# A hybrid of selective scan, attention and experts on one core: the scan's input product moved next to its scan, and PSUM divided anew

## The chip, the cores and the metric

The kernel runs on one core of a Trainium2 chip. The metric is the device time of one execution in microseconds. TensorE is called PE, VectorE DVE, ScalarE ACT and GpSimd POOL in the profile; SP is the engine that issues most of the loads. PSUM, the memory into which PE writes, has eight banks here of 128 partitions x 512 float32.

## The reference

Four images of 384 channels and 32 x 32 points pass through two layers. The first is a group norm and a selective scan along four directions (rows, columns, and both reversed), followed by a layer norm over channels, a GELU and a residual. The second takes the 1024 points as tokens: causal attention with one head of 384, then four experts of which two are taken for each token, each behind a layer norm and with a residual. The change touches the scan alone:

```python
x_dbl = jnp.einsum('bkdl,kcd->bkcl', xs, x_proj_weight)
dts, Bs, Cs = (x_dbl[:, :, :R], x_dbl[:, :, R:R + N], x_dbl[:, :, R + N:])
dts = jnp.einsum('bkrl,kdr->bkdl', dts, dt_projs_weight)
dt = jax.nn.softplus(dts + dt_projs_bias[None, :, :, None])

def step(h, inp):
    dtt, ut, bt, ct = inp
    dA = jnp.exp(dtt[..., None] * A)
    h = h * dA + (dtt * ut)[..., None] * bt[:, :, None, :]
    y = jnp.einsum('bkdn,bkn->bkd', h, ct)
    return (h, y)
```

There are B = 4 images, K = 4 directions, D = 384 channels, N = 16 states and L = 1024 steps, all in float32.

## The kernel before

**Units.** A unit of the scan holds 32 channels x 4 states on the 128 partitions, and all 1024 steps along the free dimension. It is named by image b, direction k, block m of 128 channels, quarter q of the states and j, a block of 32 channels in m: 4 x 4 x 3 x 4 x 4 = 768 units. j runs innermost, so four units in a row have the same b, k, m and q; they share one tile bc, in which B and C of four states are spread over the partitions, and their results meet in one set of matmuls. Two directions (0 and 2, or 1 and 3) make a stage of 96 units; there are two for each image, eight in all.

**What a unit does.** `front` (line 263) has ScalarE compute da = exp(dt * A) (line 268) and VectorE the product v = (dt * u) * B (line 270), which goes into PSUM, two banks for each v. `middle` (line 279) is VectorE's scan, h = da * h + v along the steps (line 282); directions 2 and 3 run it backwards. `back` (line 288) has GpSimd multiply h by C in place (line 290). Behind the fourth unit of a group it issues eight short matmuls, four for each half of the steps (the profile shows two instructions for each), that add the states up into y (line 299), in PSUM, two banks. When a block m of a stage is complete, `evict` has VectorE add y to the image's tile yb (lines 366 and 372).

**The order.** `push` (line 312) writes the order out by hand. Called with unit t it runs `front` of t, then `back` of t-2, then `middle` of t-1:

```python
flow.append(t)
done = front(t) if t is not None else None
if len(flow) > 2 and flow[-3] is not None:
    back(flow[-3], done)
if len(flow) > 1 and flow[-2] is not None:
    middle(flow[-2], done)
```

`done` is VectorE's product of unit t. `order` puts two edges: GpSimd's product of t-2 waits for it by a semaphore ("beside a scan"), and the scan of t-1 stands behind it in VectorE's queue without a semaphore ("the next unit's product first"). So VectorE runs v of t, scan of t-1, v of t+1, scan of t, and GpSimd's product of t-2 lies beside the scan of t-1. Two calls of `push(None)` empty the pipeline at the end.

The framework's scheduler turns this program into one queue for each engine. It follows these edges and the edges of data, places the rest by its own model, and puts in every semaphore; an operation that waits for several engines gets separate semaphore instructions of the engine's sequencer ahead of it.

**Preparation.** While a stage runs, the next one is prepared in small pieces: `todo` is a list of functions, and one is called after every eighth unit (line 393). `project_x` computes x_dbl for a direction (six matmuls, line 214, and copies by ScalarE, line 217); `project_dt` computes dt for a block m (two matmuls, line 229, two softplus on ScalarE, line 232, and dt * u on VectorE, line 233) and stores both to DRAM from ScalarE's queue (line 234). SP reads them back spread over four partitions each (dt4 and du4, line 246, six buffers each), and bc likewise (line 257, three buffers). `groupnorm` and `finish` (layer norm, GELU, residual) of an image are pieces too. All their PSUM tiles come from the pool `ps_m`, one bank each, by the tag "pm".

**Buffers.** da has three, h eight, bc three. PSUM's eight banks are divided among y (one tile of two banks), v (two tiles of two banks) and `ps_m` (two tiles of one bank).

Of the kernel before, what the change touches and what calls it, by code (L numbers as in the profile page):

```python
# [12 lines left out]
PSUM = bass.MemoryType.PSUM  # L13
# [27 lines left out]
def hybrid_kernel(  # L41
# [59 lines left out]
    with ExitStack() as ph:  # L101
# [6 lines left out]
        dap = ph.enter_context(tc.tile_pool(name="s_da", bufs=3))  # L108
        scr = ph.enter_context(tc.tile_pool(name="s_scr", bufs=4, space=DRAM))
        ps_y = ph.enter_context(tc.tile_pool(name="s_psy", bufs=1, space=PSUM))  # L110
        ps_b = ph.enter_context(tc.tile_pool(name="s_psb", bufs=2, space=PSUM))
        ps_m = ph.enter_context(tc.tile_pool(name="s_psm", bufs=2, space=PSUM))

        def load_x(b):
            xn = one.tile([P, M, L], F32, tag="xn", name=f"xn_{b}")
# [147 lines left out]
        def front(t):  # L263
            b, k, m, q, j = t["at"]
            g = m * NJ + j
            name = t["name"] = f"{b}_{k}_{g}_{q}"
            t["da"] = dap.tile([P, L], F32, tag="da", name=f"da_{name}")
            nc.scalar.activation(t["da"], t["dt4"], AF.Exp, scale=a4[:, k * NG + g, q : q + 1])  # L268
            t["v"] = ps_b.tile([P, L], F32, tag="v", name=f"v_{name}")
            return nc.vector.tensor_tensor(t["v"], t["du4"], t["bc"][:, 0, :], ALU.mult)  # L270

        def order(ins, after, how, reason):
            if after is not None:
                tc.add_manual_dep(
                    ins.ins, after.ins.name,
                    mybir.DependencyInfo(how, mybir.DependencyReason.DATA), reason=reason,
                )

        def middle(t, after):
            step = -1 if t["at"][1] >= 2 else 1  # L280
            t["h"] = hp.tile([P, L], F32, tag="h", name=f"h_{t['name']}")
            scan = nc.vector.tensor_tensor_scan(  # L282
                t["h"][:, ::step], t["da"][:, ::step], t["v"][:, ::step], 0.0,
                op0=ALU.mult, op1=ALU.add,
            )
            order(scan, after, mybir.DependencyClass.NoSync, "the next unit's product first")

        def back(t, after):
            h, j = t["h"], t["at"][4]
            product = nc.gpsimd.tensor_tensor(h, h, t["bc"][:, 1, :], ALU.mult)  # L290
            order(product, after, mybir.DependencyClass.Sync, "beside a scan")
            done_h.append(h)
            if j == NJ - 1:

                first = None
                for half in range(NH):
                    s = bass.ts(half, 512)
                    for jj in (NJ - 1, *range(NJ - 1)):
                        mm = nc.tensor.matmul(  # L299
                            t["y"][jj * DJ : (jj + 1) * DJ, s], sel, done_h[jj][:, s],  # L300
                            start=t["first"], stop=t["last"], tile_position=(0, jj * DJ),
                        )
                        order(mm, first, mybir.DependencyClass.NoSync, "one row of matmuls")
                        first = mm
                done_h.clear()
            if t["then"] is not None:
                t["then"]()

        flow = []
        done_h = []  # L310

        def push(t):

            flow.append(t)
            done = front(t) if t is not None else None
            if len(flow) > 2 and flow[-3] is not None:
                back(flow[-3], done)
            if len(flow) > 1 and flow[-2] is not None:
                middle(flow[-2], done)

        state = {}

# [36 lines left out]
        for si, (b, pair) in enumerate(stages):  # L359
# [18 lines left out]
            for m in range(M):  # L378
                y = ps_y.tile([P, L], F32, tag="y", name=f"y_{b}_{pair}_{m}")
                for k in PAIRS[pair]:  # L380
                    dt4 = [spread_dt(b, k, m * NJ + j) for j in range(NJ)]
                    for q in range(NQ):
                        bc = spread_bc(b, k, m, q)
                        for j in range(NJ):
                            last = k == PAIRS[pair][1] and q == NQ - 1
                            push(dict(
                                at=(b, k, m, q, j), dt4=dt4[j][0], du4=dt4[j][1], bc=bc, y=y,
                                first=k == PAIRS[pair][0] and q == 0, last=last,
                                then=(lambda m=m, y=y, f=evict: f(m=m, y=y))
                                if last and j == NJ - 1 else None,  # L390
                            ))
                            count += 1
                            if count % 8 == 4 and todo:
                                todo.pop(0)()
        push(None)
        push(None)
        for f in todo:
            f()
# [5 lines left out]
    with ExitStack() as ph:  # L404
# [4 lines left out]
        ps_m = ph.enter_context(tc.tile_pool(name="a_psm", bufs=2, space=PSUM))  # L409
# [104 lines left out]
    with ExitStack() as ph:  # L514
# [4 lines left out]
        ps_m = ph.enter_context(tc.tile_pool(name="f_psm", bufs=1, space=PSUM))  # L519
# [193 lines left out]
```

## Time and profile before

| | us |
|---|---|
| median of two runs | 5710.09 (5709.13 to 5711.04) |
| the profiled execution | 5708.17 |
| its span | 5706.4 |
| up to the first units of the scan | 62 |
| scan stage | 2926 |
| last image's finish | 64 |
| attention | 498 |
| experts | 2156 |

The five stretches are cut at 62, 2988, 3052 and 3550 us of the span, by eye from the timeline. Over the span PE is busy for 3614.5 us, VectorE for 3239.4, GpSimd for 1928.0 and ScalarE for 1656.5. In the scan stage VectorE is busy for 2883.53 of 2926 us, GpSimd for 1801.85, ScalarE for 1249.82 and PE for 987.46, at a granted PE clock of 0.58.

In the profile, a group of instructions is named by its line, engine and operation and by the tiles that it writes and reads; behind that stand the number of instructions, their busy time and the mean of one in ns, then the idle time of the engine just before them and what ended most of it. The timeline lists start and duration of single instructions in microseconds. An operation that is held up in the middle, by a port that another engine holds, counts as busy for all of that time. "DVEq" or "POOLq" is an engine's sequencer, which waits for semaphores and hands operations to the engine.

### The profile page before, as it was taken

The page shows a single profiled execution, that of the slowest core. Times are in us where ns is not written, and L with a number is a line of the kernel's source. Part 1 is how long each engine was busy: PE and PEld are TensorE (multiplying, and loading weights), DVE is VectorE, ACT ScalarE, POOL GpSimd, SP SyncE. Part 2 cuts the span into 40 slices and gives each one's busy share as a digit, 9 for nine tenths or more (in the row PEclk, how much of TensorE's full clock was granted, in tenths as well). Part 3 has the DMA queues.
Part 4 walks back from the last instruction along what each step waited for, and adds up shares of the span by engine and source line. Part 5 has one row for each costly group of instructions (what it writes and reads, how often), then busy time and mean ns, then how long its engine had stood idle before and what let it go on. Part 6 is the DMA issues. An engine that isn't in the chain of part 4 may idle for free.

```text
span 5706.4 us, 29398 instructions
## 1 busy us (share of the span) xinstructions
PE 3614.5 (63%) x10144; PEld 1443.3 (25%) x10144; DVE 3239.4 (57%) x2174; ACT 1656.5 (29%) x1709; POOL 1928.0 (34%) x872
## 2 busy tenths in 40 slices
PE   5324333243342432422227998799999999999999
PEld 1001000010000100100003444444444444444444
DVE  6999999999999999999993332300000000000000
ACT  4435435344353453543321211111111111111111
POOL 3665656656556566566660000000000000000000
PEclk7556565565565655655558999699999999999999
DMA  6444435345344444444321001000000000000000
GB/s 212 155 162 160 153 136 203 137 164 181 125 179 175 145 168 158 155 165 159 127 103 53 11 11 66 1 0 0 0 33 0 0 33 0 0 0 6 11 11 17
DMA packets 149695, 510.62 MB, mean 89 GB/s; under 512 B 21661, under 2 KB 29725, under 8 KB 148521
## 3 DMA queue, kind: packets, MB, share of 16 engines
q1 hardware_dynamic: 124544, 442.55, 22.1%
q10 hardware_dynamic: 25000, 66.19, 3.1%
q8 instruction: 79, 1.29, 0.1%
q14 instruction: 72, 0.58, 0.0%
HBM read 443.68 MB, written 65.01 MB: 89 GB/s over the span
## 4 chain that ended last, share of the span: by engine, by line
PE 46%; DVE 35%; issue 13%; DMA 3%; ACT 1%; POOL 1%; SPq 0%; DVEq 0%; ACTq 0%; POOLq 0%
DVE h L282 28%; PE ph L605 17%; PE fy L631 17%; DVE v L270 4%; PE pqk L447 2%; PE po L504 2%; PE ss L474 2%; DMA du<-dts 1%; PE pv L459 1%; POOL h L290 1%; DMA bc<-rows 1%; PE var_ff L90 1%; PE pg L553 1%; DMA dt<-dts 1%; DVE dt L233 1%
## 5 line engine op out<-in xcount | busy, mean ns | idle before, releaser
L290 POOL TENSOR_TENSOR h<-h,bc 128x1024 f32<-128x1024 f32 x768 | 1808.0, 2354 | 1184.8 <-DVE v L270 1147.0
L299 PE MATMUL y<-h,sel 128*32 128x512 f32 x3072 | 679.1, 1026 | 1704.0 <-POOL h L290 1703.8
L282 DVE TENSOR_TENSOR_SCAN h<-da,v 128x1024 f32<-128x1024 f32 x768 | 1746.1, 2274 | 1.2 <-ACT da L268 1.2
L268 ACT ACTIVATE da<-dt,a 128x1024 f32<-128x1024 f32 x768 | 881.2, 1148 | 1608.6 <-DVE h L282 1583.5
L638 DVE SCALAR_TENSOR_TENSOR fo<-fy,b2s,tw 128x512 f32<-128x512 f32 x96 | 72.1, 751 | 1837.6 <-PE fy L631 1817.8
L270 DVE TENSOR_TENSOR v<-du,bc 128x1024 f32<-128x1024 f32 x768 | 1045.5, 1361 | 32.0 <-DMA du<-dts 8.7
L605 PE MATMUL ph<-fxn,w1s 128*128 128x512 f32 x2304 | 1053.8, 594 | 0.0
L631 PE MATMUL fy<-ht,w2s 128*128 128x512 f32 x2304 | 1051.5, 593 | 0.0
L641 POOL TENSOR_TENSOR t<-t,fo 128x512 f32<-128x512 f32 x96 | 118.9, 1267 | 2539.2 <-DVE fo L638 2539.2
L610 ACT ACTIVATE ht<-ph,b1s 128x512 f32<-128x512 f32 x384 | 263.8, 687 | 1737.9 <-PE ph L605 1737.9
L299 PEld LDWEIGHTS y<-h,sel 128*32 128x32 f32 x3072 | 113.0, 156 | 2234.1 <-POOL h L290 1986.2
L605 PEld LDWEIGHTS ph<-fxn,w1s 128*128 128x128 f32 x2304 | 439.5, 191 | 551.1 <-issue 551.1
L631 PEld LDWEIGHTS fy<-ht,w2s 128*128 128x128 f32 x2304 | 436.3, 190 | 534.7 <-issue 534.7
L229 PE MATMUL pdt<-xd,wdt 12*128 12x512 f32 x192 | 163.5, 956 | 134.8 <-ACT dt L232 117.1
L447 PE MATMUL pqk<-axn,wqkv 128*128 128x512 f32 x288 | 132.9, 623 | 13.9 <-DVE axn L94 13.9
L268 ACT ACT_TABLE_LOAD x100 | 128.3, 1283 | 5.6 <-DVE yb L338 3.9
L232 ACT ACT_TABLE_LOAD x88 | 112.9, 1283 | 11.3 <-DVE dt L233 5.5
L229 PEld LDWEIGHTS pdt<-xd,wdt 12*128 12x128 f32 x192 | 42.5, 267 | 268.2 <-ACT dt L232 214.9
L504 PE MATMUL po<-pt,vt 128*128 128x512 f32 (+3 forms) x288 | 101.2, 502 | 1.6 <-DVE t L508 1.6
L474 PE MATMUL ss<-kt,qt 128*128 128x512 f32 (+3 forms) x288 | 100.7, 487 | 0.0
L447 PEld LDWEIGHTS pqk<-axn,wqkv 128*128 128x128 f32 x288 | 57.5, 201 | 89.3 <-issue 89.3
L454 DVE COPY kt<-pqk 128x512 f32<-128x512 f32 x24 | 16.6, 692 | 108.9 <-PE pqk L447 108.9
(117 smaller groups left out, 1575.2 us busy)
## 6 DMA issues: line engine op xcount, KB each, us to landing
bc<-rows SPq DMA_DIRECT2D x384, 512.0 KB, 4.5
dt<-dts SPq DMA_DIRECT2D x192, 512.0 KB, 5.9
du<-dts SPq DMA_DIRECT2D x192, 512.0 KB, 5.7
dts<-dt ACTq DMA_DIRECT2D x48, 1024.0 KB, 4.4
w1s<-in_w SPq DMA_DIRECT2D x4, 2304.0 KB, 9.0
w2s<-in_w SPq DMA_DIRECT2D x4, 2304.0 KB, 9.2
xn<-in_x SPq DMA_DIRECT2D x4, 1536.0 KB, 6.6
xr<-in_x ACTq DMA_DIRECT2D x12, 512.0 KB, 4.1
```

The lines of the kernel that those rows point to most:

```text
L229: nc.tensor.matmul(ps, wdt[:, k, m * P : (m + 1) * P], xd[:R, s], start=True, stop=True)
L268: nc.scalar.activation(t["da"], t["dt4"], AF.Exp, scale=a4[:, k * NG + g, q : q + 1])
L270: return nc.vector.tensor_tensor(t["v"], t["du4"], t["bc"][:, 0, :], ALU.mult)
L282: scan = nc.vector.tensor_tensor_scan(t["h"][:, ::step], t["da"][:, ::step], t["v"][:, ::step], 0.0, op0=ALU.mult, op1=ALU.add,)
L290: product = nc.gpsimd.tensor_tensor(h, h, t["bc"][:, 1, :], ALU.mult)
L299: mm = nc.tensor.matmul(t["y"][jj * DJ : (jj + 1) * DJ, s], sel, done_h[jj][:, s], start=t["first"], stop=t["last"], tile_position=(0, jj ...
L447: nc.tensor.matmul(ps, wqkv[:, j, c, m * P : (m + 1) * P], xn[:, c, s], start=(c == 0), stop=(c == M - 1),)
L474: nc.tensor.matmul(ss[:, o:e], qt[:, c, i * P : (i + 1) * P], kt[:, c, o:e], start=(c == 0), stop=(c == M - 1),)
L504: nc.tensor.matmul(po[:, o:], vt[:, j, m * P : (m + 1) * P], pt[:, j, o:], start=(j == 0), stop=(j == nj - 1),)
L605: nc.tensor.matmul(ph_, w1s[:, c, f * P : (f + 1) * P], xn[:, c, h * 512 : (h + 1) * 512], start=(c == 0), stop=(c == M - 1),)
L610: nc.scalar.activation(ht, ph_, AF.Gelu, bias=b1s[:, e, f : f + 1])
L631: nc.tensor.matmul(acc["y"][m], w2s[:, f, m * P : (m + 1) * P], ht, start=(f == 0), stop=(f == NF - 1),)
```

## The change

The pool of v gets one buffer in place of two, and the pool of the preparation gets the two banks: four in place of two. With one buffer the product of unit t+1 overwrites what the scan of unit t reads, so it can't be issued ahead of that scan, and `push` is rewritten: called with unit t it runs `front` of t, `back` of t-1 and `middle` of t itself, with no edge for the scan's place in the queue. GpSimd's product of t-1 still waits for VectorE's product of t. One call of `push(None)` at the end is enough.

VectorE's order becomes v of t, scan of t, v of t+1, scan of t+1; GpSimd's product of t-1 lies beside the scan of t. No operation is added or removed, and the sizes are the same.

```diff
-        ps_b = ph.enter_context(tc.tile_pool(name="s_psb", bufs=2, space=PSUM))
-        ps_m = ph.enter_context(tc.tile_pool(name="s_psm", bufs=2, space=PSUM))
+        ps_b = ph.enter_context(tc.tile_pool(name="s_psb", bufs=1, space=PSUM))
+        ps_m = ph.enter_context(tc.tile_pool(name="s_psm", bufs=4, space=PSUM))
...
             flow.append(t)
             done = front(t) if t is not None else None
-            if len(flow) > 2 and flow[-3] is not None:
-                back(flow[-3], done)
             if len(flow) > 1 and flow[-2] is not None:
-                middle(flow[-2], done)
+                back(flow[-2], done)
+            if t is not None:
+                middle(t, None)
...
         push(None)
-        push(None)
```

## The prediction

> **What bounds the kernel now.** I read the stretches first, then the groups of the scan stage, then its timeline unit by unit, and last the chain at its end. The table by stretch gives the scan stage 2926 of 5706 us, with VectorE busy for 2883.53 of them; attention and the experts behind it (498 and 2156 us, PE at 457 and 2113) hold nothing that the change edits.
>
> ```profile
> 62.00:2988.00 2926.00, 987.46 (x3584) 216.91 (x3584) 2883.53 (x1684) 1249.82 (x1116) 1801.85 (x766) 0.58 0.45 158
> ```
> ```profile
> L290 POOL TENSOR_TENSOR h<-h,bc 128x1024 f32<-128x1024 f32 x768 | 1808.0, 2354 | 1184.8 <-DVE v L270 1147.0
> L282 DVE TENSOR_TENSOR_SCAN h<-da,v 128x1024 f32<-128x1024 f32 x768 | 1746.1, 2274 | 1.2 <-ACT da L268 1.2
> L270 DVE TENSOR_TENSOR v<-du,bc 128x1024 f32<-128x1024 f32 x768 | 1045.5, 1361 | 32.0 <-DMA du<-dts 8.7
> ```
>
> The columns of the first row, from the table by stretch, are its bounds, length, busy time (and instructions) of PE, weight loads, VectorE, ScalarE, GpSimd, then clock and DMA; the others are groups of the page (busy, mean ns of one | idle before, releaser). VectorE looks like the bound: no wait to speak of stands before its product or its scan. The timeline of two units (start, duration; a release in brackets) says more.
>
> ```profile
> 1499.68 1.36 DVE L270 TENSOR_TENSOR v<-du,bc 128x1024 f32<-128x1024 f32 x1
> ...
> 1500.95 2.27 DVE L282 TENSOR_TENSOR_SCAN h<-da,v 128x1024 f32<-128x1024 f32 x1
> 1501.18 2.34 POOL L290 TENSOR_TENSOR h<-h,bc 128x1024 f32<-128x1024 f32 x1 [1.23 <-DVE v L270]
> 1503.26 1.35 DVE L270 TENSOR_TENSOR v<-du,bc 128x1024 f32<-128x1024 f32 x1
> ...
> 1506.84 1.35 DVE L270 TENSOR_TENSOR v<-du,bc 128x1024 f32<-128x1024 f32 x1
> ```
>
> Three things. (1) A unit takes 1503.26 - 1499.68 = 3.58 us. (2) The scan starts 0.09 us *before* the product ahead of it ends (1499.68 + 1.36 = 1501.04 against 1500.95): nothing ties the two, they belong to different units. The next product starts 0.04 us *after* the scan ends, since it overwrites what that scan read. So on VectorE a neighbour that must be waited for costs 0.12 us over one that need not. (3) GpSimd's product starts 0.14 us after v ends and outlasts the scan: at 1503.26 it has 0.26 us to go. Over all units v takes 1.22 us where GpSimd is done, 1.29 with 0.19 us of overlap, 1.35 with 0.26, 1.46 with 0.37, 1.65 with 0.56: v = 1.22 + (overlap - 0.12). VectorE stands still, though "busy", until GpSimd lets go. The real loop is therefore 2.34 (GpSimd) + 1.23 (its idle time, the part of v after it lets go and the 0.14) = 3.57; the scan lies beside it. Bare VectorE work is 1.22 - 0.09 + 2.27 + 0.04 = 3.44. Of four units one costs 3.685: the first with a new bc, before which GpSimd checks two more semaphores (idle time 1.32). A group of four is 3 x 3.577 + 3.685 = 14.42 us, 192 times.
>
> **The change, part by part.**
>
> *Scan t right behind its own product.* No operation is added; v of unit t moves behind scan t-1, and only the neighbours differ. Between v and scan there now is a dependence, so -0.09 becomes a gap s, and VectorE's loop is 1.22 + s + 2.27 + 0.04 = 3.53 + s. GpSimd's loop stays 3.57: the product of t-1 still waits for v of t and still lies beside a scan. The larger loop wins, so s is free up to 0.04 and costs in full above.
>
> How large is s? The trace's records of the semaphore instructions show that every scan already waits for a PE count (release of its h buffer) in a separate sequencer step, and for ScalarE's da on the instruction itself; one in four waits for GpSimd too. None waits for its own v: the next product's wait covered that. The last scan, behind which no product follows, does: its separate step holds VectorE's count and PE's together. So after the change the wait for v sits in the sequencer's step ahead of every scan, not on the instruction. Such steps are dear when nothing covers them:
>
> ```profile
> 68.70 0.02 DVEq L270
> 68.72 0.04 issue
> 68.76 0.06 DVE v L270
> ```
> ```profile
> 2985.60 1.47 DVE v L270
> 2987.07 0.02 issue
> 2987.09 0.02 POOLq L290
> 2987.11 0.09 issue
> 2987.20 6.96 POOL h L290 x3
> ```
>
> In the chain of waits, VectorE needs 0.04 from the end of its step to the start of the operation; v's count is seen 0.02 to 0.04 after v's end; a step with two semaphores takes 0.05 where the trace has one. So s = 0.03 + 0.05 + 0.04 = 0.12. A scan with a fourth wait has a second step, 0.06 to 0.07 more by GpSimd's rows (its two steps lie 0.06 apart). Bounds: at least 0.04, the plain wait between scan and v (below that the scan would read an unfinished product); at most 0.24, what GpSimd needs with three steps. I take 0.12, from VectorE's own rows.
>
> Queued behind the waiting scan on VectorE: the next product, and behind that GpSimd's product and ScalarE's da, all of which move with it.
>
> Sum for a group at s = 0.12: two units of 3.65 (+0.075 each), the one with the fourth wait 3.72 (+0.14), and the first with a new bc, where GpSimd still outlasts the scan: it ends 0.24 + 2.36 = 2.60 after v, the next v starts at 0.12 + 2.31 = 2.43, overlap 0.17, v 1.27, unit 3.70 (+0.015). Together +0.305, times 192 = **+59 us**.
>
> The Trainium skill speaks against this cost: "VectorE: DVE Perf Modes", section "The DRAIN you can't avoid", says that a semaphore between chained VectorE operations costs nothing extra. By that rule the scan would follow its product as closely as a stranger, GpSimd's loop would stay the bound, and the sum for the units would be 0. The trace's 0.04 against -0.09 speaks for the measurement.
>
> *One unit less in flight.* At the end three GpSimd products run after the last v (6.96 us); now it is two: -2.3 us. At the start the first scan (65.80) waits behind the second product, which waits for a DMA (64.66); it can now run at 62.5, and one product and scan leave the path: about -3.
>
> *Operations put between units* (42 products of dt, 24 additions of y): each lengthens GpSimd's idle time from 1.23 to about 2.37 (1.14), and in a loop bound by VectorE costs 1.26 - 0.07 - 0.08 - 0.04 = 1.07: -0.07 x 66 = -5 us. One that lands between v and its scan even hides s.
>
> *ScalarE's da* has three buffers before and after; da of t waits for scan t-3, and three products and two scans lie between the two either way, some 8.4 us. Its 1.15 us with a softplus and two table loads (1.28 + 0.69 + 1.28) fits: 0. If it did not, the row of VectorE waiting for da (1.2 us now) would show it.
>
> *The queues.* SP's bc loads follow GpSimd's fourth product of a group (1507.13 against its end at 1507.10); that stays, with one product less between v and release. The order of SP's issues, and ScalarE's store of dts, are as before; GpSimd issues no DMA. 0.
>
> *Four banks for the preparation.* PE waits 117 us for ScalarE before the dt matmuls. PE is busy for a third of this stage and nothing on VectorE waits for it there; at the start some 2 us may go (two copies of x_dbl wait 2.40 and 2.00 for PE). I count 0, bounds -5 and 0. Two softplus halves may then share their table loads; ScalarE has room, 0.
>
> Sum: +59 - 2 - 3 - 5 = +49. The profiled execution took 5708.17 us (span 5706.4); the median of the two runs is 1.9 higher. 5710 + 49, rounded: **5760 us**, 0.9% slower. About 2% is what a measurement of this kernel can tell from no change, so this counts as "within".
>
> **Rivals.**
>
> *A, forecast (0.62):* s between 0.08 and 0.18: 5735 to 5800.
>
> *B, not slower (0.22):* the wait for v costs the plain 0.04, or the order of waits puts it on the instruction. Then 3.57 = 3.57, GpSimd stays the bound, and only the short ends count: 5710 - 10 = 5700, up to 5735. For it: every dependent pair on VectorE with one wait has 0.03 to 0.04. Against: the last scan's record. It decides as long as s stays under 0.04.
>
> *C, slower by over 2% (0.13):* VectorE pays GpSimd's price, 0.24, for the step. Units 3.77, 3.77, 3.84 and 3.77: +0.73 x 192 = +140, less 10: 5840. It passes 2% (5824) from s = 0.22. Against: VectorE's 0.04 after a step where GpSimd shows 0.09.
>
> *D (0.03):* another order of the prepared operations hides s or drops GpSimd's blocking, and a unit falls towards 3.44: 768 x 0.13 = -100, about 5610. Against: the dependence needs s in nearly every unit.
>
> The range leaves out most of C and D and the edge of B: 5700 to 5820. Faster by over 2%: 0.03, all of D. Slower: C and a little of A's edge, 0.14. Within: 0.83.
>
> **What would show it.** v to scan: +0.10 to +0.13 instead of -0.09 (B: +0.04). Mean of v: 1.36 down to about 1.24, since GpSimd is done before v starts; VectorE's busy time falls by some 80 us while the stage grows. Unit period 3.65, with 3.70 and 3.72 once each in four. GpSimd's idle time before its product 1.23 up to about 1.31. Last product train 4.6 us instead of 6.96. It is wrong if da, a DMA or y's matmuls appear as the release of a VectorE wait in the scan stage, or if the scan (2.27) changes its length.

## The result, and the profile after

The changed kernel takes 5766.93 us where the kernel before takes 5710.09: a ratio of 1.010, with a 95% interval from 1.0056 to 1.0143. It is about 1% slower. The prediction said 5760, within 5700 to 5820. The profiled execution took 5766.93 us, with a span of 5765.1.

Two views of the changed kernel answer to those shown of the kernel before. First the table by stretch, cut where the same work begins and ends (columns as before), of which the scan stage is one row.

```profile
62.00:3053.00 2991.00, 977.35 (x3576) 215.46 (x3576) 2852.85 (x1683) 1246.75 (x1112) 1816.08 (x767) 0.58 0.44 154
```

The stage has grown from 2926 to 2991 us; the stretches behind it, cut by eye like those before, differ little (63, 495 and 2154 us against 64, 498 and 2156). Then the groups of the page.

```profile
L290 POOL TENSOR_TENSOR h<-h,bc 128x1024 f32<-128x1024 f32 x768 | 1819.5, 2369 | 1235.6 <-DVE v L270 1204.1
L282 DVE TENSOR_TENSOR_SCAN h<-da,v 128x1024 f32<-128x1024 f32 x768 | 1755.6, 2286 | 93.8 <-DVE v L270 2.4
L270 DVE TENSOR_TENSOR v<-du,bc 128x1024 f32<-128x1024 f32 x768 | 948.6, 1235 | 25.9 <-DMA du<-dts 1.6
```

Two figures have moved. VectorE's product is shorter, 1235 ns in place of 1361, without any change to the operation. And VectorE now stands idle before its scans, for 93.8 us in place of 1.2; only 2.4 of these have a releaser by name, since each piece is small. The timeline shows such a piece in every unit.

```profile
1509.15 1.23 DVE L270 TENSOR_TENSOR v<-du,bc 128x1024 f32<-128x1024 f32 x1
1510.52 2.29 DVE L282 TENSOR_TENSOR_SCAN h<-da,v 128x1024 f32<-128x1024 f32 x1
1510.53 2.35 POOL L290 TENSOR_TENSOR h<-h,bc 128x1024 f32<-128x1024 f32 x1 [1.23 <-DVE v L270]
1512.84 1.23 DVE L270 TENSOR_TENSOR v<-du,bc 128x1024 f32<-128x1024 f32 x1
```

The unit takes 1512.84 - 1509.15 = 3.69 us (3.58 before). The product ends at 1510.38 and its scan starts 0.14 later; before, another unit's scan started 0.09 before the product's end. GpSimd now runs from 1510.53 to 1512.88, 0.04 past the start of the next product, and holds nothing up any more. What fills the gap is named by the chain of waits, which lists start, length and engine of what the end depends on ("issue" is time in which the profile shows nothing that is waited for):

```profile
1509.15 1.24 DVE v L270
1510.40 0.03 issue
1510.43 0.05 DVEq L282
1510.48 0.04 issue
1510.52 2.30 DVE h L282
1512.82 0.02 issue
1512.84 1.24 DVE v L270
```

After the product's end come 0.03 us until the sequencer sees it, 0.05 for the sequencer's step with the semaphores of VectorE and PE, and 0.04 until the scan starts. Before, the same chain went from scan to scan over an "issue" of 1.24 us in place of the product, with no step between product and scan:

```profile
1499.68 0.03 DVE v L270
1499.71 1.24 issue
1500.95 2.28 DVE h L282
```

The trace has 897 of these steps ahead of the scans in place of 620; 611 of them hold two semaphores, in place of 152.

### The profile page after: what moved, and what is told of

Read it like the earlier page. It is cut to its first block, busy times and chain, and to the rows that moved or that the text cites. A ratio compares the mean times of both kernels' runs of the same rounds, so it can differ in the third digit from the quotient of the medians.

```text
span 5765.1 us, 29659 instructions
## 1 busy us (share of the span) xinstructions
PE 3602.4 (62%) x10144; PEld 1438.9 (25%) x10144; DVE 3207.7 (56%) x2174; ACT 1651.0 (29%) x1705; POOL 1939.6 (34%) x872
## 3 DMA queue, kind: packets, MB, share of 16 engines
q8 instruction: 79, 1.29, 0.1%
## 4 chain that ended last, share of the span: by engine, by line
DVE 47%; PE 45%; issue 4%; DMA 2%; ACT 1%; DVEq 1%; POOL 0%; ACTq 0%; SPq 0%; POOLq 0%
DVE h L282 28%; PE ph L604 17%; PE fy L630 17%; DVE v L270 16%; PE pqk L446 2%; PE po L503 2%; PE ss L473 2%; PE pv L458 1%; PE var_ff L90 1%; PE pg L552 1%; DVE dt L233 1%; DVEq L282 1%; PE pw L622 0%; PE var_at L90 0%; DMA xr<-in_x 0%
## 5 line engine op out<-in xcount | busy, mean ns | idle before, releaser
L282 DVE TENSOR_TENSOR_SCAN h<-da,v 128x1024 f32<-128x1024 f32 x768 | 1755.6, 2286 | 93.8 <-DVE v L270 2.4
L270 DVE TENSOR_TENSOR v<-du,bc 128x1024 f32<-128x1024 f32 x768 | 948.6, 1235 | 25.9 <-DMA du<-dts 1.6
```

Of the source, the lines that this page charges most:

```text
L282: scan = nc.vector.tensor_tensor_scan(t["h"][:, ::step], t["da"][:, ::step], t["v"][:, ::step], 0.0, op0=ALU.mult, op1=ALU.add,)
```

## The experiments

The theory: the cost is the wait of the scan for its own product, which now lies ahead of every scan in the sequencer, less what VectorE lost to GpSimd in the kernel before. The rivals: the cost is the order as such, with no product done ahead, so that operands come late; the new division of PSUM costs; GpSimd's later start costs. All ratios are to runs of the kernel before on the same chip as the experiment.

### The wait alone

The kernel before, with its order and its buffers. One word is changed, so that the edge that has only ordered the queue now carries a semaphore.

```diff
-            order(scan, after, mybir.DependencyClass.NoSync, "the next unit's product first")
+            order(scan, after, mybir.DependencyClass.Sync, "the next unit's product first")
```

> The old order and the old two buffers of v, but the edge that puts the scan of t-1 behind the product of t is turned into one with a semaphore, so that every scan waits for VectorE's count ahead of it, as it does in the changed kernel. Theory (the wait ahead of the scan is the whole cost): the gap from product to scan goes from -0.09 to +0.13 us, the unit from 3.58 to about 3.69, the time to 5767 + 5 (the unit that the old order keeps in flight at both ends) = 5772, range 5760 to 5780. Rival (the cost is that the product is no longer a unit ahead, so that operands come late): the order is the old one, 5710. Rival (the new division of PSUM): 5710.

Measured: 5770.95 us against 5710.62, a ratio of 1.0103 (1.0088 to 1.0118). The timeline of this kernel has the unit of the changed one:

```profile
1511.81 1.23 DVE L270 TENSOR_TENSOR v<-du,bc 128x1024 f32<-128x1024 f32 x1
...
1513.17 2.29 DVE L282 TENSOR_TENSOR_SCAN h<-da,v 128x1024 f32<-128x1024 f32 x1
1513.18 2.35 POOL L290 TENSOR_TENSOR h<-h,bc 128x1024 f32<-128x1024 f32 x1 [1.24 <-DVE v L270]
1515.49 1.23 DVE L270 TENSOR_TENSOR v<-du,bc 128x1024 f32<-128x1024 f32 x1
```

The gap is 0.13 us and the unit 3.68, although this scan doesn't read the product that it waits for, the product is still a unit ahead, and PSUM is divided as before. The wait by itself makes a loss of the same size, 60 us.

### The new order with two buffers of v

The order of the changed kernel, without what one buffer brings with it: the product does not overwrite what the scan in front of it reads. An edge without semaphore keeps it behind that scan.

```diff
-        ps_b = ph.enter_context(tc.tile_pool(name="s_psb", bufs=1, space=PSUM))
-        ps_m = ph.enter_context(tc.tile_pool(name="s_psm", bufs=4, space=PSUM))
+        ps_b = ph.enter_context(tc.tile_pool(name="s_psb", bufs=2, space=PSUM))
+        ps_m = ph.enter_context(tc.tile_pool(name="s_psm", bufs=2, space=PSUM))
...
+            order(product, t["behind"], mybir.DependencyClass.NoSync, "behind the scan before")
```

> The new order, but two buffers of v again (and two banks for the preparation), with an edge without semaphore that keeps each product behind the scan before it. The scan waits for its own product as in the changed kernel; the product need not wait for the scan in front any more. Theory: product to scan stays at +0.13, scan to product goes from +0.04 to -0.08, VectorE's unit is 1.23 + 0.13 + 2.29 - 0.08 = 3.57, and GpSimd's loop of 3.58 is the bound again, with v drawn out to about 1.35. 663 units at 3.58 in place of 3.685, and the shorter ends stay: 5767 - 67 = 5700, range 5690 to 5715. Rival (the order itself, with no product ahead, is the cost): 5767.

Measured: 5698.69 us, 0.9979 of the kernel before (0.9969 to 0.9989).

```profile
1509.68 1.25 DVE L270 TENSOR_TENSOR v<-du,bc 128x1024 f32<-128x1024 f32 x1
...
1511.06 2.29 DVE L284 TENSOR_TENSOR_SCAN h<-da,v 128x1024 f32<-128x1024 f32 x1
1511.07 2.35 POOL L293 TENSOR_TENSOR h<-h,bc 128x1024 f32<-128x1024 f32 x1 [1.23 <-DVE v L270]
1513.26 1.24 DVE L270 TENSOR_TENSOR v<-du,bc 128x1024 f32<-128x1024 f32 x1
```

The gap before the scan is there (1510.93 to 1511.06), but the next product starts at 1513.26, 0.09 before the scan's end at 1513.35. Over all pairs the scan starts 0.128 us behind its product, as in the changed kernel, and the next product 0.082 before the scan's end, where the changed kernel has 0.035 behind it: VectorE gets 0.12 us of each unit back. Its chain is then 1.233 + 0.131 + 2.286 - 0.082 = 3.57 us, just inside GpSimd's loop of 1.23 + 2.35 = 3.58, which is the unit again (3.579 on the median; the mean is 3.597 against 3.583 before). Since the two loops are so nearly equal, the product is hardly drawn out: 1.266 us on the mean, where 1.35 was expected. The new order as such costs nothing in the time. What the changed kernel lacks is one neighbour on VectorE that need not be waited for.

### Two banks for the preparation

```diff
-        ps_m = ph.enter_context(tc.tile_pool(name="s_psm", bufs=4, space=PSUM))
+        ps_m = ph.enter_context(tc.tile_pool(name="s_psm", bufs=2, space=PSUM))
```

> The changed kernel with two banks for the preparation in place of four; two banks stay unused. Theory: 5767, range 5760 to 5775, since nothing on VectorE waits for the preparation's banks; at the start some 2 us may come back. Rival (the four banks change the scheduler's order of the preparation and that costs or saves time): below 5750 or above 5780.

Measured: 5770.37 us, a ratio of 1.0102 (1.0087 to 1.0117), within the interval of the changed kernel. The four banks neither cost nor save anything that can be told from the time. They do go with another order at the start of the scan, to which the account of the prediction comes back.

### Both kernels without GpSimd's product

```diff
-            product = nc.gpsimd.tensor_tensor(h, h, t["bc"][:, 1, :], ALU.mult)
-            order(product, after, mybir.DependencyClass.Sync, "beside a scan")
```

From the kernel before:

> The kernel before without GpSimd's product: the states are not multiplied by C and are added up as the scan left them (this part of the computation is left out). Theory (in the kernel before, VectorE's product stands still until GpSimd lets go): v 1.22 throughout, the unit 1.22 - 0.09 + 2.27 + 0.04 = 3.44 instead of 3.58, 663 x 0.14 = 93, and some 7 us at the end: 5610, range 5590 to 5625. Rival (VectorE's own work is the bound, GpSimd lies beside it): 5703, only the end is shorter.

From the changed kernel:

> The changed kernel without GpSimd's product (the same part of the computation is left out). Theory (in the changed kernel the scan's wait leaves GpSimd the time, and VectorE's chain of product, wait and scan is the bound): the unit stays at 3.69, only the end is some 5 us shorter: 5762, range 5745 to 5768, and the distance to the kernel before without GpSimd is 663 x 0.25 = 165 us or a little less. Rival (GpSimd still holds VectorE up, or the loss comes through GpSimd's later start): it falls by about 90 as well, to 5670.

Measured: 5579.75 us from the kernel before, 0.9773 of it (0.9754 to 0.9793), and 5751.03 from the changed kernel, 1.0073 (1.0053 to 1.0093). A unit of the kernel before without GpSimd:

```profile
1505.01 1.23 DVE L270 TENSOR_TENSOR v<-du,bc 128x1024 f32<-128x1024 f32 x1
...
1506.16 2.28 DVE L282 TENSOR_TENSOR_SCAN h<-da,v 128x1024 f32<-128x1024 f32 x1
...
1508.47 1.23 DVE L270 TENSOR_TENSOR v<-du,bc 128x1024 f32<-128x1024 f32 x1
```

and one of the changed kernel without it:

```profile
1503.01 1.23 DVE L270 TENSOR_TENSOR v<-du,bc 128x1024 f32<-128x1024 f32 x1
...
1504.38 2.29 DVE L282 TENSOR_TENSOR_SCAN h<-da,v 128x1024 f32<-128x1024 f32 x1
1506.70 1.23 DVE L270 TENSOR_TENSOR v<-du,bc 128x1024 f32<-128x1024 f32 x1
```

The unit falls from 3.58 to 3.46 in the one and stays at 3.69 in the other. So GpSimd sets the pace of the kernel before, unseen behind a VectorE that counts as busy, and does not set that of the changed kernel; its later start there is not what costs, either. The distance between the two, 171 us, is the price of the wait without the cover: 767 steps of a unit x (3.683 - 3.457) us, the means of the units with nothing put between, is 173.

The first of the two expectations was missed: 5580 where the range ended at 5590. The units gave what was expected, 767 x (3.583 - 3.457) = 97 us. The operations put between units gave another 29: with a product of dt in it, a unit takes 4.96 us on the mean in the kernel before and 4.55 without GpSimd, a difference of 0.41 and not the 0.14 of a bare unit.

### h as one tile for a group of four, in the kernel before

A test of the price of a step on the other engine. With h in one tile for four units, three of four GpSimd products have one semaphore to wait for, which the instruction can carry itself.

```diff
-        hp = ph.enter_context(tc.tile_pool(name="s_h", bufs=8))
+        hp = ph.enter_context(tc.tile_pool(name="s_h", bufs=2))
...
-            t["h"] = hp.tile([P, L], F32, tag="h", name=f"h_{t['name']}")
+            j = t["at"][4]
+            if j == 0:
+                group_h.append(hp.tile([P, NJ, L], F32, tag="h", name=f"h_{t['name']}"))
+            t["h"] = group_h[-1][:, j, :]
```

> The kernel before, with h as one tile for the four units of a group (two buffers of four in place of eight of one). PE's release then has to be waited for once in a group, and in three of four units GpSimd's product waits for VectorE's count alone, on the instruction, without a separate step of the sequencer. Theory (GpSimd's loop is the bound of the kernel before, and a separate step costs about 0.05 us where nothing covers it): v's end to GpSimd's start 0.14 to 0.09, the unit from 3.58 to 3.53 in three of four, 576 x 0.05 = 29 us: 5681, range 5670 to 5695. Rival (VectorE's own instructions are the bound, GpSimd lies beside them): 5710.

Measured: 5672.65 us, 0.9934 of the kernel before (0.9919 to 0.9949).

```profile
1510.72 1.29 DVE L270 TENSOR_TENSOR v<-du,bc 128x1024 f32<-128x1024 f32 x1
...
1511.92 2.27 DVE L285 TENSOR_TENSOR_SCAN h<-da,v 128x1024 f32<-128x1024 f32 x1
1512.09 2.35 POOL L293 TENSOR_TENSOR h<-h,bc 128x1024 f32<-128x1024 f32 x1 [1.17 <-DVE v L270]
1514.23 1.29 DVE L270 TENSOR_TENSOR v<-du,bc 128x1024 f32<-128x1024 f32 x1
```

GpSimd starts 0.08 us after the product's end in place of 0.14, its idle time is 1.17 in place of 1.23, and the unit 3.51 in three of four (one in four, before which GpSimd has more to wait for, stays at 3.68). Product to scan is as before, -0.085 on the mean, so it isn't VectorE's own wait that moved. GpSimd outlasts the scan by 0.06 less, so the next product is shorter too: 1.29. A wait of GpSimd that VectorE's own row never showed was worth 38 us of the kernel's time, where 29 were expected.

### h as one tile, in the changed kernel

The same edit in the changed kernel.

> The changed kernel with h as one tile for a group of four units. In three of four units the sequencer's step ahead of the scan holds VectorE's count alone, in place of VectorE's and PE's. Theory (VectorE's chain is the bound, and a step with one semaphore takes 0.02 in place of 0.05): product to scan 0.13 to 0.10 in those, 576 x 0.03 = 17: 5750, range 5743 to 5758; GpSimd's earlier start, worth 38 us in the kernel before, is worth nothing here. Rival (GpSimd's loop counts here too): 5730.

Measured: 5759.68 us, a ratio of 1.0089 (1.0074 to 1.0104). This was 2 us above the expected range, and the interval overlaps that of the changed kernel; the size is read from the trace instead.

```profile
L285 DVE TENSOR_TENSOR_SCAN h<-da,v 128x1024 f32<-128x1024 f32 x768 | 1756.0, 2286 | 79.7 <-DVE v L270 1.8 <-ACT da L268 1.2
L270 DVE TENSOR_TENSOR v<-du,bc 128x1024 f32<-128x1024 f32 x768 | 951.6, 1239 | 25.4 <-DMA du<-dts 1.0
```

The idle time before the scans falls from 93.8 to 79.7 us, since the usual gap goes from 0.13 to 0.10 with one semaphore in the step; 3 us are lost again in the product, which now meets GpSimd's end once in a group. From the first product to the last the profiled execution gains 11 us (2980.4 in place of 2991.7), of the 17 expected; behind GpSimd's last product, where the edit changes nothing, it loses 8 (2716.5 in place of 2708.7), and why is open. That GpSimd's earlier start brings nothing here fits these numbers, as the theory has it; the rival's 5730 is outside the interval.

### Both: two buffers, the new order, h as one tile

> The new order with two buffers of v, and h as one tile for a group of four. VectorE's unit is 1.23 + 0.10 + 2.29 - 0.08 = 3.54, GpSimd's 3.51 and once in four 3.68: the larger one each time. Theory: three of four units go from 3.58 to 3.54, 576 x 0.04 = 23 us below the new order with two buffers alone: 5676, range 5668 to 5690, level with the kernel before with grouped h (5672.65) or a little above. Rival (GpSimd's loop alone sets the time): 5665.

Measured: 5673.68 us, 0.9936 of the kernel before (0.9919 to 0.9952).

```profile
1508.75 1.21 DVE L270 TENSOR_TENSOR v<-du,bc 128x1024 f32<-128x1024 f32 x1
...
1510.04 2.34 POOL L296 TENSOR_TENSOR h<-h,bc 128x1024 f32<-128x1024 f32 x1 [1.17 <-DVE v L270]
1510.06 2.29 DVE L287 TENSOR_TENSOR_SCAN h<-da,v 128x1024 f32<-128x1024 f32 x1
1512.26 1.21 DVE L270 TENSOR_TENSOR v<-du,bc 128x1024 f32<-128x1024 f32 x1
```

By place in the group the units take 3.51, 3.52, 3.55 and 3.68 us on the median, where the kernel before with grouped h has three of 3.51 and one of 3.68 (means 3.559 and 3.539). VectorE's chain has come down to within 0.04 us of GpSimd's loop; the two versions are level in time, and both beat the two kernels of this case.

## Why the prediction was right

**The bound.** That GpSimd holds up VectorE's product was right, and removing GpSimd showed it. It also explains the product's shorter time in the changed kernel: mean 1.235 us, where 1.24 was expected; without GpSimd it is 1.233.

**The gap s.** Expected 0.12, as 0.03 + 0.05 + 0.04; the chain shows these three pieces, and the mean over 719 pairs is 0.128. The last scan of the kernel before, whose step held VectorE's count and PE's together, was the right row to read. That every scan of the kernel before had such a step was read too broadly: 620 of 768 had one, and in the changed kernel some steps hold VectorE's count alone.

**The fourth wait** was expected to add 0.06 to 0.07 in one unit of four. It adds nothing: in 146 of these 192 units PE's semaphore gets a step of its own, which the sequencer takes while the product still runs, and the step that is left is as long as the others (0.05 us). The unit is 3.69 like the rest, not 3.72. The first unit with a new bc is 3.69 too, where 3.70 was expected.

**The sum for the units** was +59 and turned out as +78: 767 x (3.685 - 3.583). The term that was mis-sized is the unit of before. The prediction took 14.42 / 4 = 3.605; the mean is 3.583, because some 80 units behind an operation that was put between take only 3.44 to 3.46 (GpSimd has finished by the time their product starts, and holds nothing up). For the unit of after it had a mean of 3.68 against 3.685, and this closeness is luck: the plain unit was put too low, 3.65 against 3.69 (product 1.235 and not 1.22, gap 0.13 and not 0.12, and the scan, which was taken as unchanged, 0.012 longer), and the fourth wait too dear.

**The operations put between** were expected to give back 5 us. Their surplus over plain units falls by 11, from 548.6 - 104 x 3.583 = 176 to 544.9 - 103 x 3.685 = 165. It is the other side of the same mis-sized term, and some 5 us of loss at the start lie in it too.

**The ends.** The last chain was right: two GpSimd products of 2.35 us in place of 6.96, and from the last v to GpSimd's end 6.1 us in place of 8.5. At the start the step failed. The first product does come earlier (58.67 in place of 61.20), but its scan, expected at 62.5, starts at 68.83: the scheduler put a product of dt between the two, which waited 6.47 us for ScalarE. This goes with the four banks, which the prediction counted as nothing: in the three kernels with the new order and two banks no such product lies there, and in the changed kernel with two banks the first scan starts at 62.22. By the eighth unit the changed kernel is 3.2 us behind (96.4 against 93.2), where it began 2.5 ahead and seven longer units explain 0.7. With two banks the eighth unit comes at 95.4, and by the last product the lead is gone (both start it at 3050.4).

**What it adds up to.** +78 - 11 between first and last v, -2.5 for the earlier first v, -2.5 at the end, and -3.5 in what follows GpSimd's last product (the last finish, attention, experts), where the change edits nothing: +58.7, the difference of the two spans. The prediction's +49 is 10 short of it (8 of the difference of the medians, 56.8): the units were put 19 too low, the operations between them gave back 6 more, and the 3.5 were not foreseen. That these partly cancel is luck, too.

**What would show it.** The gap and the product came as written; the last train takes 4.7 us where 4.6 was written, the period is 3.69 throughout in place of 3.65 with one of 3.70 and one of 3.72, and GpSimd's idle time is 1.34 in place of about 1.31. One sign of being wrong did come: the scan changed its length, from 2.274 to 2.286 us. That is 0.012 of the 0.10 us by which a unit grew, so the sum for the units is off by it, and the wait remains what makes the loss. The other signs did not come: VectorE waits 1.2 us for da, as before, 1.6 in place of 8.7 for du, and not at all for y's matmuls. VectorE's busy time was expected to fall by 80 us and fell by 32: overlapping instructions are counted once, and with the overlap between product and scan (0.085 x 737 = 63 us) gone, most of the 97 us that the product saves do not show.

**The rivals.** B, with a plain wait of 0.04, would have needed the wait on the instruction; C needed 0.22. D, a better order of the rest, did not come up. The four banks were rightly counted as nothing in the sum, though not at the start.

The Trainium skill, in "VectorE: DVE Perf Modes", section "The DRAIN you can't avoid", found for a chain of eight tensor_copy that the semaphore costs nothing extra. That does not hold for the operations here: the wait alone, with nothing else changed, cost 60 us in 768 scans, 0.08 each net of what GpSimd had cost, and 171 us, 0.22 each, is the distance without GpSimd.

## What to carry to other kernels

Two operations of VectorE that depended on each other cost more here when they were neighbours: the second started 0.035 us behind the first with the wait on the instruction and 0.13 behind it with the wait in a step of its own, but 0.085 before its end when it needn't wait. So before giving up a buffer that keeps an independent operation between two, add up the gap for both sides, scan to product and product to scan, and look whether the wait can ride on the instruction or needs a step of its own. A busy time that varies for one shape (1.21 to 1.76 us here) can be a wait in disguise; plot it against the overlap with the other engine to find the true loop. And of two loops of nearly equal length, shortening or lengthening one shows only as far as it is, or becomes, the longer: taking GpSimd's product out gave 129 us where its loop was the longer, and 16 where VectorE's was.

## What was not expected

The scan itself became longer when it waited for the product in front of it: 2.274 us before, 2.286 or 2.287 in the changed kernel and with the wait alone, 2.287 without GpSimd too (2.279 in the kernel before without GpSimd). So it comes with the wait, with or without GpSimd; but 0.005 of the 0.012 came without the wait, when GpSimd's product was left out. Why is open.

A few scans start not 0.13 but about 0.48 us behind their product: five in the changed kernel with VectorE's product as the named releaser, four with the wait alone, eight without GpSimd. The engine is idle before them for 2 to 4 us in all. Their da had been ready for 7.9 us or more and their step had ended as usual, and no run here tells what they wait for.

The number of semaphores in one step matters: the step takes 0.05 us with two and 0.02 with one, and the usual gap from product to scan is 0.13 and 0.10.
